# Issuing the stores of q*v from GpSimd's queue in place of SyncE's

## Chip, cores and metric

The kernel runs on one core of a Trainium2 chip. The metric is the device time of one execution in microseconds (us). The engines are TensorE (PE; its weight loads are PEld), VectorE (DVE), ScalarE (ACT), GpSimd (POOL) and SyncE (SP). SyncE computes nothing; it issues DMAs. The traces write a queue of a DMA-issuing engine as SPq, ACTq or POOLq.

## The reference

The reference is a chain of four layers on x of shape (8, 56, 56, 192) in float32. Each layer normalizes x in groups and adds its result to x. Layers 0 and 1, the only ones that the change touches, are these (layer 2 is a convolution block with an MLP, layer 3 windowed attention):

```python
x = gn(x)
p = silu(x @ p_w.T + p_b)
q = silu(x @ q_w.T + q_b)          # 192 -> 576 channels
v = silu(x @ v_w.T + v_b)
qv = q * v
o1 = toeplitz(qv along w, a1)      # one decaying filter per channel
o2 = toeplitz(qv along h, a2)
x = x + (p * (o1 + o2)) @ o_w.T + o_b
```

## The kernel before

Layers 0 and 1 each have three parts, and each part is run for two halves of the batch (j0 = 0 and j0 = 2):

- `tno_qv` computes q*v from x and stores it to the DRAM tensor `qv`.
- `tno_toeplitz` reads `qv` back and applies the two filters; its result goes to the DRAM tensor `L_sum`.
- `tno_out` computes p, multiplies it by that result, applies the output matrix and writes the next x.

`weave` runs `tno_toeplitz` of one half inside the loops of `tno_qv` or `tno_out` of other work: each of these is a generator that yields after a piece of work with an estimate of its time, and the weaver lets the Toeplitz generator take a step whenever its share is due. For example `tno_toeplitz` of the first half runs within the rest of `tno_qv` of that half and `tno_qv` of the second. The stretches of the trace in which `tno_qv` runs are about 0 to 960 us, 1330 to 1760 us and 2180 to 2620 us. From about 100 us on TensorE, ScalarE, VectorE and GpSimd execute in the order in which the program gives their instructions. SyncE executes its own queue in order as well, and waits where an instruction of it must wait.

In `tno_qv` a tile of 128 tokens is worked on in units of 512, 512 and 128 columns, or 512 and 128 where one call does a part of the columns. A unit has these steps:

1. TensorE multiplies into banks (L263).
2. VectorE adds the bias and writes a tile `z` (L272). `z` has three buffers ("t8").
3. In `multiply`, ScalarE applies silu to `z` (L301).
4. In `multiply`, GpSimd forms the product of its halves in a tile `prod` (L304). `prod` has three buffers ("t4"), which `tno_out` uses too.
5. The store of `prod` to `qv` (L307). It is not issued at once: it is put into the list `stores` and called at the start of the next `multiply`, ahead of the next silu and the next product.

A store of a 512-wide unit is 512 KB, in runs of 512 bytes, eight for each of 128 tokens. All stores together are 300.

In `tno_toeplitz` SyncE loads a block of q*v in the tile `q` (L380 along w, one of its two halves from ScalarE's queue; L383 along h) and the filter matrix `tm` (L393). TensorE multiplies (L406), ScalarE copies the result to `ot` (L413, two buffers), VectorE transposes it (L424 along w, straight into the sum `s`; L426 along h). In the half-step along h, GpSimd adds the transposed result to `s` (L429, four times in a half-step; on VectorE in the last block) and issues the stores of the sum (L436, or L444 in the last block) from its own queue. The other loads that SyncE issues in these stretches are x for `tno_qv` (L240), and x (L119) and sums (L508) for `tno_out`. In the first 440 us it also loads and stores what the filters are built from (L145 to L204).

Of the kernel before, what the change touches and what calls it, by code (L numbers as in the profile page):

```python
# [43 lines left out]
class Net:  # L44
# [179 lines left out]
    def tno_qv(self, L, j0, xs, gn, qv, apart=None, cols=(0, 2 * D1), g0=0):  # L224
# [3 lines left out]
        nc, p, inp = self.nc, self.tp, self.inp  # L228
# [68 lines left out]
        def multiply(m, n, z, at, c0):  # L297
            k = n // 128
            for f in stores:
                f()  # L300
            nc.scalar.activation(z[:m, :n, :], z[:m, :n, :], AF.Silu)  # L301
            prod = p.tile([128, 4, DC * 4], F32, name="t4")
            half = z[:m, :n, :].rearrange("p (n h c) b -> p n h (c b)", h=2, c=DC)
            nc.gpsimd.tensor_mul(prod[:m, :k], half[:, :, 0], half[:, :, 1])  # L304
            n0 = c0 // 128
            stores[:] = [
                lambda: nc.sync.dma_start(  # L307
                    qv[2 * n0 : 2 * n0 + 2 * k, at : at + m, :].rearrange("n t e -> t n e"),
                    prod[:m, :k].rearrange("p n (h e) -> p (n h) e", h=2),
                )  # L310
            ]
# [7 lines left out]
        if apart:  # L319
            units = []  # L320
            for g in range(2):
                x, t0, n = loaded[g]
                for s in range(0, n, 128):
                    for c0 in range(0, 2 * D1, 512):
                        k = min(512, 2 * D1 - c0)
                        z = apart.tile([128, k, 4], F32, name=f"z{len(units)}", bufs=1)
                        units.append((x, s, 128, c0, k, z, t0 + s))
            for j in range(2):
                for g in range(2):
                    normalize(*loaded[g], (j,))  # L330
                for x, s, m, c0, k, z, at in units:
                    if late is not None:
                        multiply(*late)
                    half_unit(x, s, m, c0, k, z, j)
                    if j:
                        late = (m, k, z, at, c0)
                        if len(loaded) < 4:
                            loaded.append(load(len(loaded)))
                    yield 2.7 * k / 512
            loaded = loaded[2:]  # L340
            normalize(*loaded[0])
        else:
            yield from self.all_norms()
            normalize(*loaded[0])
        for g in range(2 if apart else g0, groups):
            x, t0, n = loaded.pop(0)
            for s in range(0, n, 128):
                m = min(128, n - s)
                for c0 in range(*cols, 512):
                    k = min(512, cols[1] - c0)  # L350

                    if late is not None:
                        multiply(*late)
                    if c0 == max(cols[0], min(512, cols[1] - 512)) and s + 128 >= n and g + 1 < groups:
                        normalize(*loaded[0])
                    z = p.tile([128, 512, 4], F32, name="t8")
                    unit(x, s, m, c0, k, z)
                    late = (m, k, z, t0 + s, c0)
                    if c0 == cols[0] and s == 0 and g + 2 < groups:
                        loaded.append(load(g + 2))  # L360
                    yield 5.3 * k / 512
        multiply(*late)
        stores[0]()

# [1310 lines left out]
```

## Time and profile before

| what | value |
|---|---|
| median of 3 runs | 5452.3 us (5446.23 to 5452.5) |
| profiled execution, time | 5448.52 us |
| profiled execution, span from the first instruction to the last | 5446.5 us |
| mean granted TensorE clock | 0.978 |
| DMA moved | 1116.48 MB |
| GpSimd busy, whole span | 1767.5 us (32%) |
| product on GpSimd (L304) | 300 instructions, 550.08 us |
| GpSimd's adds (L429), 128 of them | 550.9 us |

A row of the groups names a line of the code, the engine, the operation, the tiles written and read, the number of instructions, their busy time and the mean of one in ns; behind the second bar stands the time that the engine was idle just before them and what ended it. A row of the waits gives the total in us, the number and the longest. A row of the timeline gives start and duration in us, and in brackets the idle time before it with what ended it. A mean granted clock of 1.00 is full speed. SyncE's instructions and the issuing of DMAs from ScalarE are not counted as busy time; a DMA issue on GpSimd has a row of its own.

### The profile page before, as it was taken

To read this page: it belongs to the slowest core of one execution; us is meant where nothing else is said; L and a number is where in the kernel's file an instruction comes from. 1 tells how busy PE (TensorE), PEld (TensorE's weight loads), DVE (VectorE), ACT (ScalarE), POOL (GpSimd) and SP (SyncE) were. 2 spreads that over 40 slices of the span, in tenths; PEclk is the share of its full clock that TensorE was granted. 3 is DMA by queue.
4 is the path that set the end of the run, shared out by engine and by line. 5 is a ranking of instruction groups with operands and counts; after the bars stand their busy time and mean duration, and the time that the engine had idled before them with its cause. 6 is when DMAs were issued, how large, how long until landed. Compare 5 with 4: busy or idle time off the path is not lost.

```text
span 5446.5 us, 144346 instructions
## 1 busy us (share of the span) xinstructions
PE 5166.3 (95%) x64672; PEld 3811.3 (70%) x64672; DVE 2588.6 (48%) x3990; ACT 2384.0 (44%) x3179; POOL 1767.5 (32%) x1291
## 2 busy tenths in 40 slices
PE   7879999999999999999999899989999999999998
PEld 4657777777777777777777778855665444777776
DVE  6535556455555555645566322422212331566665
ACT  3345555444554454655454322242323333444443
POOL 2225675233664333645443100000001100333333
PEclk9889999999999999999999999999999999999999
DMA  7699997887786999888897666634444221445442
GB/s 253 149 242 280 289 315 228 274 279 256 248 267 170 327 309 308 277 233 280 296 325 246 205 219 237 221 127 161 140 165 121 74 69 49 84 97 108 99 103 68
DMA packets 1051146, 1116.48 MB, mean 205 GB/s; under 512 B 235200, under 2 KB 986304, under 8 KB 1036128
## 3 DMA queue, kind: packets, MB, share of 16 engines
q1 hardware_dynamic: 911584, 854.88, 52.7%
q0 software_dynamic: 38144, 200.99, 9.6%
q10 hardware_dynamic: 100800, 51.38, 3.7%
q8 instruction: 508, 8.32, 0.6%
q14 instruction: 110, 0.90, 0.1%
HBM read 743.17 MB, written 363.94 MB: 203 GB/s over the span
## 4 chain that ended last, share of the span: by engine, by line
PE 49%; DMA 3%; DVE 2%; issue 1%; ACT 1%; POOL 1%; SPq 1%; ACTq 0%; POOLq 0%; DVEq 0%
PE bank L976 7%; PE bank L837 5%; PE bank L1056 5%; PE bank L1250 4%; PE bank L263 3%; PE bank L592 3%; PE bank L1070 3%; PE bank L536 3%; PE bank L1366 2%; PE bank L1280 2%; PE bank L1197 2%; PE bank L1321 2%; PE bank L586 1%; PE bank L406 1%; PE bank L1340 1%
## 5 line engine op out<-in xcount | busy, mean ns | idle before, releaser
L263 PE MATMUL bank<-wq,t 128*128 128x256 f32 (+4 forms) x7680 | 1289.1, 374 | 73.5 <-DVE t L272 43.7
L263 PEld LDWEIGHTS bank<-wq,t 128*128 128x128 f32 (+2 forms) x7680 | 1004.9, 190 | 351.6 <-issue 92.5
L272 DVE TENSOR_TENSOR t<-bank,wq 128x1024 f32<-128x1024 f32 (+3 forms) x480 | 517.7, 1112 | 691.4 <-PE bank L263 540.9
L304 POOL TENSOR_TENSOR t<-t 128x1024 f32<-128x1024 f32 (+2 forms) x288 | 528.4, 1848 | 673.9 <-ACT t L301 338.5
L413 ACT COPY ot<-bank 128x896 f32<-128x896 f32 x576 | 493.2, 909 | 511.5 <-PE bank L406 401.8
L429 POOL TENSOR_TENSOR s<-s,ot 128x1568 f32<-128x1568 f32 x128 | 550.9, 4305 | 197.4 <-DVE ot L426 137.7
L301 ACT ACTIVATE t<-t 128x2048 f32<-128x2048 f32 (+2 forms) x288 | 423.2, 1488 | 330.5 <-DVE t L272 320.5
L406 PE MATMUL bank<-q,tm 56*32 56x224 f32 x18432 | 505.1, 354 | 18.7 <-DMA tm<-L_tab 11.6
L406 PEld LDWEIGHTS bank<-q,tm 56*32 56x32 f32 x18432 | 340.2, 106 | 145.3 <-issue 84.1
L122 POOL DMA_DIRECT2D x<-t x112 | 87.0, 777 | 1087.6 <-DVE t L601 1022.9
L555 ACT ACTIVATE bank<-bank,wo 128x448 f32<-128x448 f32 x448 | 262.9, 606 | 386.2 <-PE bank L545 361.2
L560 DVE TENSOR_TENSOR t<-t,bank 128x896 f32<-128x896 f32 x224 | 242.7, 1087 | 397.8 <-ACT bank L555 339.8
L976 PE MATMUL bank<-z,w 128*128 128x448 f32 (+1 forms) x1344 | 414.4, 556 | 1.5 <-ACT h L985 1.5
L536 PE MATMUL bank<-t,wo 128*128 128x224 f32 x1792 | 372.0, 361 | 21.4 <-ACT t L515 10.2
L536 PEld LDWEIGHTS bank<-t,wo 128*128 128x128 f32 x1792 | 334.9, 192 | 51.0 <-issue 30.2
L592 PE MATMUL bank<-t,wo 128*128 128x224 f32 x1792 | 368.9, 359 | 0.0
L592 PEld LDWEIGHTS bank<-t,wo 128*128 128x128 f32 x1792 | 329.9, 190 | 31.2 <-issue 31.2
L837 PEld LDWEIGHTS bank<-xt,cm 113*112 113x112 f32 x3072 | 316.1, 180 | 42.8 <-issue 33.9
L837 PE MATMUL bank<-xt,cm 113*112 113x108 f32 (+2 forms) x3072 | 324.4, 265 | 10.8 <-ACT h L985 5.7
L976 PEld LDWEIGHTS bank<-z,w 128*128 128x128 f32 (+1 forms) x1344 | 183.0, 189 | 206.7 <-issue 198.7
L127 POOL DMA_DIRECT2D x<-x x64 | 36.7, 574 | 843.4 <-DVE x L1007 813.5
L424 DVE STREAM_TRANSPOSE s<-ot 128x1792 f32<-128x1792 f32 x144 | 292.8, 2034 | 23.0 <-ACT ot L413 14.8
(162 smaller groups left out, 6972.8 us busy)
## 6 DMA issues: line engine op xcount, KB each, us to landing
q<-qv SPq DMA_DIRECT2D x36, 3584.0 KB
t<-L_sum SPq DMA_DIRECT2D x112, 1008.0 KB
L_sum<-s POOLq DMA_DIRECT2D x256, 392.0 KB, 7.3
qv<-t SPq DMA_DIRECT2D x192, 512.0 KB
cm<-in_L_cm SPq DMA_DIRECT2D x96, 896.0 KB
tm<-L_tab SPq DMA_DIRECT2D x288, 240.0 KB
q<-qv SPq DMA_DIRECT2D x40, 1568.0 KB
q<-qv ACTq DMA_DIRECT2D x32, 1568.0 KB
```

The costliest lines, as they stand in the source:

```text
L263: nc.tensor.matmul(pp[:m, b, 256 * j : 256 * j + k], x[rows, j, 2 if part else b, s : s + m], w[rows, part, c0 + c : c0 + c + k],  start=p ...
L272: nc.vector.tensor_add(z[:m, c : c + k, :], view(pp[:m], 0, [[1, k], [256, 4]]), view(bias[:m], c0 + c, [[1, k], [0, 4]]),)
L301: nc.scalar.activation(z[:m, :n, :], z[:m, :n, :], AF.Silu)
L304: nc.gpsimd.tensor_mul(prod[:m, :k], half[:, :, 0], half[:, :, 1])
L406: nc.tensor.matmul(pt[32 * j : 32 * j + 32, r, hf * 224 : (hf + 1) * 224], tm[rows, at : at + 32], q[rows, :, 4 * c : 4 * c + 4], start=Tr ...
L413: nc.scalar.copy(view(ot, 4 * (g % 4), [[16, 2], [32, 112], [1, 4]]), view(pt, 0, [[512, 2], [4, 112], [1, 4]]),)
L424: nc.vector.transpose(to, of.rearrange("p (i k) -> p i k", k=32))
L429: add.tensor_add(to, to, view(of, 0, [[1, 28], [32, 56]]))
L536: mm(gs[c // 2][:, b, c % 2 * 256 : c % 2 * 256 + N], pw[:, 0, 128 * c : 128 * c + 128], xn[:, b], start=c % 2 == 0, stop=False,)
L592: mm(P[:, b, :N], ow[:, c, 0:128], g[:, 4 * b + c], start=False, stop=c == 3)
L837: nc.tensor.matmul(pc[:, 128 * e + 4 * m0 : 128 * e + 4 * m1], cm[:113, e, k, :], xt[:, m0 - 1 + k : m1 - 1 + k, c + e, :], start=n == 0 a ...
L976: nc.tensor.matmul(phs[c][:, s, :TT], w0[rows, part, at : at + 128], z[rows, Z[2 if part else s], :], start=part == flip, stop=part != flip,)
```

## The change

The store of `prod` is issued from GpSimd's queue instead of SyncE's, for all 300 units. The place of the call in the program is the same: at the start of the next `multiply`, or at the end of `tno_qv` for the last. The data, the shapes and the buffers are the same.

```diff
             nc.gpsimd.tensor_mul(prod[:m, :k], half[:, :, 0], half[:, :, 1])
             n0 = c0 // 128
             stores[:] = [
-                lambda: nc.sync.dma_start(
+                lambda: nc.gpsimd.dma_start(
                     qv[2 * n0 : 2 * n0 + 2 * k, at : at + m, :].rearrange("n t e -> t n e"),
                     prod[:m, :k].rearrange("p n (h e) -> p (n h) e", h=2),
                 )
```

## The prediction

> **What bounds the kernel now.** I read the page's busy times and its chain first, then the waits of the engines, then SyncE's own waits, then two stretches of the timeline.
>
> ```profile
> PE 5166.3 (95%) x64672; PEld 3811.3 (70%) x64672; DVE 2588.6 (48%) x3990; ACT 2384.0 (44%) x3179; POOL 1767.5 (32%) x1291
> PE 49%; DMA 3%; DVE 2%; issue 1%; ACT 1%; POOL 1%; SPq 1%; ACTq 0%; POOLq 0%; DVEq 0%
> ...
> POOL t L304 <- DMA qv<-t: 325.1, 58, 30.4
> DVE t L272 <- POOL t L304: 138.7, 37, 23.3
> PE bank L263 <- DVE t L272: 43.7, 14, 9.7
> ...
> SPq L307 <- POOL t L304: 698.6, 199, 23.7
> ```
>
> TensorE is busy 95% of the span, so the change can win only the time in which TensorE stands still for the store, and lose only by making it stand still anew. The three waits below form one chain: the product on GpSimd (L304) waits for an old store to give back its `prod` buffer (325.1 us), VectorE's bias add (L272) waits for the product to give back `z` (138.7 us), TensorE waits for L272 to empty a bank (43.7 us). At each step most of the wait is swallowed by slack. The last line says that SyncE stands at the store for 698.6 us until the product is there, with later loads behind it.
>
> The timeline shows why the store is late, in the worst place:
>
> ```profile
> 2545.05 0.70 SPq L380 DMA_DIRECT2D q<-qv  x1
> ...
> 2545.85 14.19 SPq L307 DMA_DIRECT2D qv<-t  x2
> ...
> 2564.56 3.02 POOL L304 TENSOR_TENSOR t<-t 128x1024 f32<-128x1024 f32 x2 [11.88 <-DMA qv<-t]
> ...
> 2566.93 0.69 DVE L272 TENSOR_TENSOR t<-bank,wq 128x512 f32<-128x512 f32 x1 [9.91 <-POOL t L304]
> ...
> 2567.67 2.93 PE L263 MATMUL bank<-wq,t 128*128 128x256 f32 x6 [9.67 <-DVE t L272]
> ```
>
> SyncE issues a load of q, and two stores right behind it take 14.19 us to issue where the tile view gives a median of 365 ns. The product waits 11.88 us, VectorE 9.91, TensorE 9.67. The same picture stands behind the q loads issued at 468, 581, 645, 1412 and 2385 us; after the first two, four `tm` loads (15.30 and 12.28 us) stand between as well.
>
> The other stretch shows GpSimd with no room left, in the half-steps of the Toeplitz part that add on GpSimd:
>
> ```profile
> 745.55 8.58 POOL L429 TENSOR_TENSOR s<-s,ot 128x1568 f32<-128x1568 f32 x2
> 754.42 2.11 POOL L436 DMA_DIRECT2D L_sum<-s  x4 [0.29 <-POOL s L429]
> 756.55 5.38 POOL L304 TENSOR_TENSOR t<-t 128x1024 f32<-128x1024 f32 x3
> 758.97 2.36 DVE L272 TENSOR_TENSOR t<-bank,wq 128x1024 f32<-128x1024 f32 x2 [1.14 <-POOL t L304]
> 761.47 6.79 PE L263 MATMUL bank<-wq,t 128*128 128x128 f32 x31 [1.92 <-ACT ot L413]
> ```
>
> From 741 to 762 us GpSimd runs without a pause, three products have piled up, and VectorE just begins to wait for them (1.14 us). Anything put on GpSimd here is seen by TensorE soon.
>
> **What the change takes away.** 300 issues leave SyncE. (a) The stalls of the chain above. From the timeline I took each TensorE gap over 0.7 us in the q/v stretches and kept those whose L272 waited for a product that waited for `qv<-t`: 2.85 us at 496, 3.39 at 610, 2.87 at 666, 1.91 at 1432, 2.08 at 2404, 9.67 at 2568. Sum 22.8 us. Gaps of 5.03 at 922, 5.16 at 1699 and 1.92 at 2326 lie behind VectorE's own adds of the last block (L429 on DVE) and stay. The 7.81 us at 2614, where L515 waits for a `t4` buffer, I leave in: the last store is issued late because the last product is, and it still has to land.
> (b) In the first 440 us SyncE's stores delay loads. At 292.83 two stores take 7.64 us and the x loads go out only at 300.56; TensorE waits 6.35 us for L246 on them, and 3.90 us for the small `wo` load that shares the queue. At 378 it waits 11.65 us for `tm`, whose loads left SyncE behind six stores (340 to 347 us) and a q load. I count 6.35 + 3.90 and half of 11.65 (the q load stays): 16 us.
> (c) The granted clock is 0.95 in 2400 to 2620 us, where the two longest waits lie, 1.00 in the undisturbed slices: 5% of 220 us is 11 us, and I count 3 for one of two waits gone. Total gain 42 us.
>
> **What it adds.** GpSimd issues 300 DMAs in its own order, between one product and the next. The trace has no GpSimd issue of this form, so I bound it by rows of the groups kept apart by form:
>
> ```profile
> L122 POOL DMA_DIRECT2D x<-t x112 | 87.0, 777 | 1087.6 <-DVE t L601 1022.9 <-DVE st L604 53.2 <-DVE t L523 7.9
> L127 POOL DMA_DIRECT2D x<-x x64 | 36.7, 574 | 843.4 <-DVE x L1007 813.5 <-DVE yn L939 27.5 <-issue 2.4
> L743 POOL DMA_DIRECT2D qv<-none x2 | 2.3, 1170 | 0.0
> ```
>
> By the code L127 moves 128 runs, L122 384 (128 rows of 3) and L743 2016 (112 rows of 18). The store of a 512-wide unit has 128 x 8 = 1024 runs of 512 B, that of a 128-wide one 256. Between L122 and L743 that gives 777 + 640/1632 x 393 = 0.93 us; between L127 and L122, 0.68 us. Ends: 0.57 (cheapest row) and 1.17 us (dearest). 200 x 0.93 + 100 x 0.68 = 254 us, plus up to 0.29 us where it directly follows its own product (as L436 does above): at most 341 us on an engine with 3679 us idle. So the mean costs nothing; what counts is the half-steps without room. A half-step of some 34 us holds about six products (91 in 520 us), so six stores: 4 x 0.93 + 2 x 0.68 and some 0.29s, 5 to 6.5 us. Walking the stretch above through with them put in, the adds end 2 us later, the first piled-up product 2.9 us later, the last 5 us; then come 15 us with little to do and GpSimd catches up. The row L429 counts 66 GpSimd adds in the q/v stretches (31, 16, 7, 12), four to a half-step: 16 half-steps. In most VectorE doesn't wait there today, or by under 1 us; so of 2.9 us I let 1.1 through: 16 x 1.1 = 18 us lost. Ends: 0 (all slack) and 5 (the last product's delay): 0 to 80 us.
>
> **Where the new store lands.** GpSimd's queue holds only stores, so no q load is ahead. The page's issues give 7.3 us for L436 (392 KB) and 7.4 us for L122 (336 KB) while DMA is 80 to 97% busy; scaled, 512 KB is about 10 us. `prod` has three buffers, so a store has two units, some 14 us, before it is missed. Behind four L436 (1.57 MB, about 6 us more) it may be just late, but there the product is late anyway. I count 0; if it took 20 us, today's stalls would stay.
>
> Two rules of the Trainium skill speak against this. The first is weighed at the 14.19 us row. "DMA: Bandwidth & Descriptors", section "Issuing engines are not separate DMA queues", says that all issuers share the same 16 engines and that another issuer saves only issue time. By it (a) stays, and the sum is 18 us lost less about 10 of (b): 5460. The row shows a queue that is full behind a 1.5 MB load, which is order and not bandwidth, so I follow the row. The second is weighed at L436: "SBUF — State Buffer", section "SBUF: two separate sides", says that some VectorE copies lock GpSimd out of writing descriptors and that SyncE's transfers are immune. At 741.10 four L436 took 2.10 us while VectorE ran L426 (741.66 to 745.6), no slower than the 2.11 at 754.42; L424, L426 and L272 don't do it. By the rule each store could lose the 2.0 us of a transpose, 300 x 2 = 600 us on GpSimd; I take 0, and keep it for the upper end.
>
> **Sum.** The profiled execution has a span of 5446.5 us and a time of 5448.5, within 0.1% of the median 5452.3, so I subtract from the median: 5452.3 - 42 + 18 = 5428 us.
>
> **Rivals.**
> 1. GpSimd becomes the bound of the add half-steps. Slower: break-even is 42/16 = 2.6 us per half-step reaching TensorE. At 5 us (a half-step's last product) it is 80 - 42 = 38 us slower, 5490. For it: the 1.14 us above, 98.5 us in which ScalarE's copy L413 already waits for L429. Against: half-steps at 580 and 700 us end with GpSimd waiting for ScalarE.
> 2. Gain and loss cancel: 5441 to 5463. For it: the gain is six gaps, the loss sixteen small ones.
> 3. It does not do what it says: the store lands as late on GpSimd's queue because the engines, not the queue, are full (DMA 1.00 in 500 to 600 us). Then only (b) and the loss remain: 5452 - 10 + 18 = 5460. Against: the landing times above.
>
> **Chances.** 0.2% is 11 us, about what a measurement can tell from no change. Forecast, 5392 to 5441: 0.60. Rivals 2 and 3 within 11 us: 0.15. Rival 1, with the tail of rival 3: 0.25. The forecast's own range is 5400 to 5441; to hold 8 in 10 the range takes in rival 2 and half of rival 1: 5395 to 5480.
>
> **What would show it.** Right: POOL L304 <- DMA qv<-t falls from 325 to under 60 us; the gaps at 496, 610, 666, 1432 and 2568 are gone; GpSimd's busy time rises by about 250 us; the row of the new issue is 0.9 us; DVE L272 <- POOL L304 has more, shorter waits. Wrong: an issue of 2 us or more; ACT L413 <- POOL L429 far above 98.5 us with TensorE gaps of 3 us or more in each add half-step; or waits for `qv<-t` still at 300 us.

## Result and profile after

| | before | after |
|---|---|---|
| median | 5452.4 us (4 runs, 5446.23 to 5456.65) | 5478.18 us (4 runs, 5468.96 to 5483.71) |
| ratio | | 1.0051 (95% interval 1.0038 to 1.0063) |
| profiled execution: time, span | 5448.52, 5446.5 us | 5468.96, 5466.8 us |
| mean granted TensorE clock | 0.978 | 0.974 |
| GpSimd busy | 1767.5 us | 2033.9 us |

The change makes the kernel slower by 26 us (21 to 34 by the interval), where 24 us faster was forecast. Ratios, here and below, are to the kernel before on the same chip. The page of the changed kernel, first its busy times, then the chain that ended last by engine:

```profile
PE 5179.8 (95%) x64672; PEld 3820.1 (70%) x64672; DVE 2591.8 (47%) x3990; ACT 2383.8 (44%) x3179; POOL 2033.9 (37%) x1591
PE 74%; POOL 6%; DMA 6%; DVE 5%; issue 4%; ACT 3%; SPq 1%; POOLq 0%; ACTq 0%; DVEq 0%
```

GpSimd has 266 us and 300 instructions more. The chain covers the whole span here and only 58% of it before, so these shares can't be set side by side. The waits (total in us, number, longest) say more. First two rows of the kernel before:

```profile
ACT ot L413 <- POOL s L429: 98.5, 34, 7.9
PE bank L536 <- ACT t L515: 10.2, 3, 7.8
```

Then the changed kernel:

```profile
ACT ot L413 <- POOL s L429: 155.4, 41, 10.8
DVE t L272 <- POOL t L304: 133.3, 38, 6.4
POOL t L304 <- DMA qv<-t: 84.0, 36, 5.1
POOL qv L307 <- POOL t L304: 59.7, 191, 0.9
PE bank L263 <- DVE t L272: 27.6, 16, 4.0
PE bank L536 <- ACT t L515: 19.9, 2, 10.1
```

The chain that the prediction wanted to cut is cut: the product waits 84.0 us for old stores where it waited 325.1, VectorE's longest wait for a product is 6.4 us and was 23.3, TensorE's wait for VectorE fell from 43.7 to 27.6 us. Two rows stand against that. ScalarE's copy L413 waits 155.4 us for GpSimd's adds (98.5 before). And in the last row TensorE stands twice, 10 us each time, for L515, the normalization of an x tile in `tno_out`. Before, this wait had one long stand, the 7.81 us at 2614 us that the prediction left in; the two of 10 us are at other places, where the prediction looked for no wait.

The issue itself cost what was estimated. The groups kept apart by form:

```profile
L307 POOL DMA_DIRECT2D qv<-t x300 | 258.3, 861 | 76.8 <-POOL t L304 59.7 <-issue 7.9 <-DMA qv<-t 3.1
```

258 us against 254, and the wait for the own product (59.7 us over 191 issues) is the 0.3 us of the L436 row.

The queue is not all that changed. Two DMA queues of the page (packets, MB, share of the 16 engines' span), first before, then after:

```profile
q1 hardware_dynamic: 911584, 854.88, 52.7%
q0 software_dynamic: 38144, 200.99, 9.6%
```

```profile
q1 hardware_dynamic: 680992, 739.26, 44.9%
q0 software_dynamic: 71168, 316.62, 16.2%
```

The 115.6 MB of the stores left q1 in 230592 packets of about 0.5 KB and came to q0 in 33024 of about 3.5 KB. What the larger packets are worth, apart from the queue, no run tells. In e7 below the stores keep the small packets on a third queue, and the product's wait for them is 140.1 us, far under 325.1 as well, though in a kernel that is held up elsewhere.

The place that the prediction showed first, where two stores took 14.19 us to issue behind a q load, looks like this in the timeline after (start, duration, in brackets the idle time before):

```profile
2568.29 0.33 SPq L380 DMA_DIRECT2D q<-qv  x1
2568.68 14.86 SPq L393 DMA_DIRECT2D tm<-L_tab  x4
...
2573.31 0.93 POOL L307 DMA_DIRECT2D qv<-t  x1 [0.30 <-POOL t L304]
2579.06 0.71 POOL L304 TENSOR_TENSOR t<-t 128x256 f32<-128x256 f32 x1 [4.82 <-DMA qv<-t]
```

The load is as before, and it is now the `tm` loads that stand 14.86 us in SyncE's queue behind it. The store is issued in its own 0.93 us, and what is left of the stall is smaller: the product still waits 4.82 us for a landing, and TensorE stands 3.51 us at 2581 in place of 9.67.

The other stretch, in an add half-step:

```profile
749.19 8.51 POOL L429 TENSOR_TENSOR s<-s,ot 128x1568 f32<-128x1568 f32 x2
...
757.73 1.71 ACT L413 COPY ot<-bank 128x896 f32<-128x896 f32 x2 [8.43 <-POOL s L429]
...
764.09 1.69 ACT L413 COPY ot<-bank 128x896 f32<-128x896 f32 x2
...
765.03 5.30 PE L263 MATMUL bank<-wq,t 128*128 128x128 f32 x24 [3.21 <-ACT ot L413]
```

The trace lags by 3.6 us here, and so do the two adds (749.19, 745.55 before). ScalarE waits 8.43 us for the first of them to free `ot`, its next copy comes at 764.09, and TensorE stands 3.21 us (1.92 before). Eight such gaps of 1.7 to 3.2 us are in the q/v stretches, 19.0 us together; before there is only this one of that size. A ninth, of 7.31 us at 2638 us, is no added loss: it stands where the 7.81 us for L515 stood at 2614 us. L515 doesn't wait there any more, and an add is late instead. All of TensorE's waits for L413 in front of L263, before and after:

```profile
PE bank L263 <- ACT ot L413: 5.9, 14, 1.9
PE bank L263 <- ACT ot L413: 17.3, 20, 3.2
```

**Where the time went.** I aligned the traces by ScalarE's instructions, which stand in one order in all kernels of the table below, and took the difference of their start times to the kernel before, as the median of nine neighbours. The table gives by how much that difference grew in a part. The part behind 2985 us (layers 2 and 3) is left out: no edit touches it, and it moved by -0.1 to +9.2 us from one kernel to another. The table sets single executions, on more than one chip, against one of the kernel before. How good a cell is shows in e11, which has the queues of the kernel before: outside the transitions its cells are 2.8, 4.1 and -2.7. So a cell is good to some 5 us, and the ratios decide on sums.

| kernel | startup, to 440 us | three q/v stretches | two transitions to `tno_out` | rest | at 2985 us |
|---|---|---|---|---|---|
| changed kernel | 6.5 | -5.0 | 18.1 | 0.6 | 20.2 |
| e1_startup_sync | 6.4 | 6.0 | 18.3 | 0.0 | 30.7 |
| e2_xn_in_place | 10.9 | 2.2 | 1.7 | 3.4 | 18.2 |
| e3_both | 5.2 | 1.8 | 1.0 | 3.9 | 11.9 |
| e4_filler | 10.2 | 37.0 | 4.1 | 2.4 | 53.7 |
| e5_sync_in_adds | 10.3 | -25.9 | 0.5 | 0.9 | -14.2 |
| e6_filler_behind | 3.9 | 27.5 | 2.9 | 0.9 | 35.2 |
| e9_sync_start_adds | 3.1 | -24.3 | 3.6 | -0.3 | -17.9 |
| e10_gpsimd_in_adds | 1.6 | 39.8 | 1.3 | 1.1 | 43.8 |
| e11_before_xn_late | 2.8 | 4.1 | 20.0 | -2.7 | 24.2 |

The q/v stretches, of which the prediction treats at length, are no slower in the changed kernel. The loss lies at the two transitions and, less clear of the 5 us, in the startup.

### The profile page after: what moved, and what is told of

The parts are those of the page before. It is cut to its first block, busy times and chain, and to the rows that moved or that the text cites. A ratio compares the mean times of both kernels' runs of the same rounds, so it can differ in the third digit from the quotient of the medians.

```text
span 5466.8 us, 144138 instructions
## 1 busy us (share of the span) xinstructions
PE 5179.8 (95%) x64672; PEld 3820.1 (70%) x64672; DVE 2591.8 (47%) x3990; ACT 2383.8 (44%) x3179; POOL 2033.9 (37%) x1591
## 4 chain that ended last, share of the span: by engine, by line
PE 74%; POOL 6%; DMA 6%; DVE 5%; issue 4%; ACT 3%; SPq 1%; POOLq 0%; ACTq 0%; DVEq 0%
PE bank L263 13%; PE bank L976 7%; PE bank L592 6%; PE bank L536 6%; PE bank L837 5%; PE bank L406 5%; PE bank L1056 5%; PE bank L1250 4%; DMA qv<-t 3%; PE bank L586 3%; PE bank L1070 3%; POOL t L304 3%; PE bank L545 2%; POOL s L429 2%; PE bank L1366 2%
## 5 line engine op out<-in xcount | busy, mean ns | idle before, releaser
L263 PE MATMUL bank<-wq,t 128*128 128x256 f32 (+4 forms) x7680 | 1292.6, 375 | 68.2 <-DVE t L272 27.6
L263 PEld LDWEIGHTS bank<-wq,t 128*128 128x128 f32 (+2 forms) x7680 | 1006.9, 190 | 348.2 <-issue 91.3
L272 DVE TENSOR_TENSOR t<-bank,wq 128x1024 f32<-128x1024 f32 (+3 forms) x480 | 517.7, 1112 | 691.8 <-PE bank L263 535.0
L413 ACT COPY ot<-bank 128x896 f32<-128x896 f32 x576 | 493.2, 909 | 540.4 <-PE bank L406 364.1
L429 POOL TENSOR_TENSOR s<-s,ot 128x1568 f32<-128x1568 f32 x128 | 551.3, 4308 | 203.2 <-DVE ot L426 137.2
L536 PE MATMUL bank<-t,wo 128*128 128x224 f32 x1792 | 373.6, 362 | 25.9 <-ACT t L515 19.9
L536 PEld LDWEIGHTS bank<-t,wo 128*128 128x128 f32 x1792 | 337.1, 193 | 54.8 <-issue 27.4
```

What stands on the lines that cost most here:

```text
L263: nc.tensor.matmul(pp[:m, b, 256 * j : 256 * j + k], x[rows, j, 2 if part else b, s : s + m], w[rows, part, c0 + c : c0 + c + k],  start=p ...
L272: nc.vector.tensor_add(z[:m, c : c + k, :], view(pp[:m], 0, [[1, k], [256, 4]]), view(bias[:m], c0 + c, [[1, k], [0, 4]]),)
L413: nc.scalar.copy(view(ot, 4 * (g % 4), [[16, 2], [32, 112], [1, 4]]), view(pt, 0, [[512, 2], [4, 112], [1, 4]]),)
L429: add.tensor_add(to, to, view(of, 0, [[1, 28], [32, 56]]))
L536: mm(gs[c // 2][:, b, c % 2 * 256 : c % 2 * 256 + N], pw[:, 0, 128 * c : 128 * c + 128], xn[:, b], start=c % 2 == 0, stop=False,)
```

## Experiments

**The transitions.** At 960 us in the changed kernel:

```profile
959.58 0.34 SPq L380 DMA_DIRECT2D q<-qv  x1
960.04 0.73 POOL L307 DMA_DIRECT2D qv<-t  x1 [0.30 <-POOL t L304]
970.82 1.50 ACT L515 ACTIVATE t<-t,gn 128x224 f32<-128x224 f32 x3 [8.86 <-DMA qv<-t]
971.44 4.10 PE L536 MATMUL bank<-t,wo 128*128 128x224 f32 x10 [10.13 <-ACT t L515]
```

L515 wants a "t4" buffer for the second x tile. It is the last but one product's, whose store (256 KB) was issued 0.46 us behind a q load and landed some 10.5 us later; the median of all stores is 6.5 us in the tile view of `qv`. At 1770 us it is the same (9.79 us). Before, L515 waited for nothing at this place:

```profile
954.98 1.49 ACT L515 ACTIVATE t<-t,gn 128x224 f32<-128x224 f32 x3
```

The addresses in the built programs tell why: in the kernel before, that tile has the buffer of the first x tile, which TensorE has just read; in the changed kernel it has the buffer of the last but one product. Which free buffer of the pool a tile gets is decided when the program is built, and moving the stores changed that decision. At the third transition, near 2614 us, the decision changed the other way: before, the second x tile had a product's buffer (the 7.81 us), now it has that of the first x tile. So there are two causes to tell apart, the late landing and the placing. e2_xn_in_place restores the placing and leaves all stores on GpSimd:

```diff
-        def normalize(j, x):
-            xn = p.tile([128, 3, N], F32, name="t4")
+        def normalize(j, x, xn=None):
+            xn = xn or p.tile([128, 3, N], F32, name="t4")
...
-            xn = normalize(*after) if after else None
+            xn = normalize(*after, None if before else xn) if after else None
```

> The changed kernel with all 300 stores on GpSimd, but at each transition from Q to O the second normalized x tile (L515) is written into the buffer of the first, as the kernel before has it placed, and not into that of the last but one product. Theory (the PE gaps of 10.13 us at 971 and 9.79 us at 1770 are a wait for that product's store, which the changed kernel's placing of buffers made): both gaps go, 18 to 20 us less than the changed kernel, 5458 to 5460. Rival 1 (GpSimd's store and the loads around it land late whatever waits for them): the gaps are then L406 or L536 waiting for q or for s instead, gain under 5 us. Rival 2 (GpSimd's own time is the loss): no gain, 5477 to 5479.

Measured: ratio to the kernel before 1.0026 (1.0016 to 1.0035), 14 us slower, where the changed kernel has 1.0051. The two transitions cost 1.7 us in place of 18.1. ScalarE's timeline at the same place:

```profile
969.60 1.49 ACT L515 ACTIVATE t<-t,gn 128x224 f32<-128x224 f32 x3
```

It waits for nothing. The theory holds: about half of the loss comes from this wait. (14 us above the kernel before is more than the 6 to 8 us expected; the startup and the q/v stretches of this execution are worse than the changed kernel's by 11.6 us in the table, without an edit there.)

The opposite, e11_before_xn_late: the kernel before, all stores on SyncE, with the changed kernel's placing.

```diff
+            self.prods = [*getattr(self, "prods", [])[-1:], prod]
...
+            last = self.prods[0].rearrange("p n c -> p (n c)")[:, : 3 * N].rearrange("p (k n) -> p k n", k=3)
-            xn = normalize(*after) if after else None
+            xn = normalize(*after, None if before or not woven else last) if after else None
```

> The kernel before with all stores on SyncE, and one edit: at each transition from Q to O the second normalized x tile is written into the buffer of the last but one product, where the changed kernel has it. Theory (the two gaps of 10 us are made by the placing of that tile, whoever begins the store): gaps of 8 to 10 us at L536 <- ACT L515 near 956 and 1750 us here too, 16 to 20 us above the kernel before. Rival (the store lands late only because GpSimd begins it behind the q load): SyncE's store is in time, 0 to 4 us above it.

Measured: 1.0020 (1.0013 to 1.0028), 11 us slower; the transitions cost 20.0 us in the table. TensorE's timeline of this kernel:

```profile
971.35 6.31 PE L537 MATMUL bank<-t,wo 128*128 128x224 f32 x16 [11.45 <-ACT t L516]
```

The gap is there with SyncE's stores too, at 956 us on the clock of the kernel before, and again ahead of 1773 us (L516 waits 9.53 us). So it comes with the placing, whoever begins the store. By the ratio it comes to less than the 16 to 20 us expected, and I don't explain that difference.

**The startup.** The products of the twelve first units fall into one stretch, and in the changed kernel GpSimd has no pause in it. GpSimd's timeline at the end of the stretch, first of the kernel before:

```profile
97.84 0.10 POOL L149 MEMSET L0pw<- 128x1 f32 x1
101.78 2.38 POOL L304 TENSOR_TENSOR t<-t 128x1024 f32<-128x1024 f32 x1 [3.84 <-issue]
```

Then of the changed kernel:

```profile
103.63 0.93 POOL L307 DMA_DIRECT2D qv<-t  x1 [0.30 <-POOL t L304]
104.58 0.74 POOL L304 TENSOR_TENSOR t<-z 128x256 f32<-128x256 f32 x1
105.24 0.11 POOL L149 MEMSET L0pw<- 128x1 f32 x1
```

The kernel before is done with these units and the first memset L149 by 97.94 us and then stands 3.84 us idle; the changed kernel gets to that memset at 105.24, 7.4 us later. The filter tables hang behind it on VectorE, and L272 behind those. e1_startup_sync gives the stores of these units back to SyncE, in fact of eleven: the twelfth is issued outside this loop, and the trace has 289 stores on GpSimd.

```diff
-        def multiply(m, n, z, at, c0):
+        def multiply(m, n, z, at, c0, by=nc.gpsimd):
...
-                        multiply(*late)
+                        multiply(*late, by=nc.sync)
                     half_unit(x, s, m, c0, k, z, j)
```

> The changed kernel, but the stores of the twelve units of the startup section are again begun by SyncE; the other 288 stay on GpSimd. Theory (the change loses in separate places: about 8 us in the startup, where GpSimd runs without a pause and each store's issue and the wait for its own product put off the memsets of the decay tables behind it; about 20 us at two transitions from Q to O; some 1 to 2 us in each of the add half-steps): 8 us less than the changed kernel, near 5470 us. Rival 1 (each GpSimd issue costs the same wherever it stands, 26 us over 300): 12 of 300 are worth 1 us, 5477. Rival 2 (the startup is bound by the loads, and what is won there is waited for again at tm<-L_tab at 386 us): 5476 to 5478.

Measured: 1.0039 (1.0026 to 1.0052), not separable from the changed kernel. The trace shows why: at 150 us the lag is 2.8 us in place of 8.5, but at 378 us it is 7.5 and 8.0. The later startup units have their stores on GpSimd still, and the lag is there again; that they make it is likely, and e9 below fits it. e3_both joins the two edits:

> Both edits together: the twelve startup stores by SyncE, and the second normalized x tile written into the first one's buffer; 288 stores on GpSimd. Theory: the two losses are in separate places and add, 26 to 28 us less than the changed kernel, 5450 to 5453, level with the kernel before; what then remains of the loss in the add half-steps (about 15 us) balances the removed stalls. Rival (one of the two only moves the wait): 5458 to 5470. That the removed stalls are worth the predicted 23 us net of the half-steps would be 5440 or less.

Measured: 1.0022 (1.0015 to 1.0029), 12 us slower than the kernel before. That can't be told from e2's 1.0026: the miss is the startup term, which these eleven stores don't decide.

**GpSimd's time without the queue.** e4_filler keeps SyncE's stores and puts a useless memset ahead of each product:

```diff
+            nc.gpsimd.memset(prod[:m, : 4 if k > 1 else 3], 0.0)
             half = z[:m, :n, :].rearrange("p (n h c) b -> p n h (c b)", h=2, c=DC)
```

> The kernel before with its stores on SyncE, and on GpSimd ahead of each product a memset of the product's tile (about 0.97 us for a unit 512 wide, 0.73 for one 128 wide, 300 in all, some 267 us), which computes nothing; the second normalized x tile is written into the first one's buffer, as the kernel before places it. It has the GpSimd time of the change without its queue. Theory: the startup loss of about 8 us and the half-steps' 10 to 18 us appear, the stalls of 23 us behind the q loads stay, no wait of 10 us at the transitions: 5465 to 5478, that is 13 to 25 us above the kernel before. Rival 1 (GpSimd's time is the whole of the loss, and more by what the removed stalls brought): 5490 to 5500. Rival 2 (GpSimd's time is hidden, the loss is the queue's): 5450 to 5456.

Measured: 1.0093 (1.0076 to 1.0109), 51 us slower, far over the theory's 13 to 25 and over the 38 to 48 of rival 1 too. But this filler lies between the landing of an old store and the product, and so makes each of today's stalls longer. e6_filler_behind has it where the change has its issue:

```diff
+        scr = p.tile([128, 256], F32, name="scr", bufs=1)
...
             for f in stores:
                 f()
+                for turn in range(3 if n > 128 else 2):
+                    nc.gpsimd.memset(scr, 0.0)
```

> The kernel before, stores on SyncE; on GpSimd, where the change issues the store, three memsets of 128x256 (two for a unit 128 wide) of a tile of their own that nothing reads, about 0.9 us, 300 times; second normalized x tile in the first one's buffer. Against e4_filler the filler no longer stands between the landing of an older store and the product. Theory (GpSimd's time as such costs some 45 us, and the move of the stores to another queue gives 30 of them back): 35 to 50 us above the kernel before. Rival (e4's 51 us was mostly the longer way from landing to product in the stalls behind the q loads, and the half-steps cost what was predicted): 15 to 25 us above it.

Measured: 1.0055 (1.0042 to 1.0067), 30 us slower, between the two expectations. The group of the filler, and a row of the waits:

```profile
L303 POOL MEMSET scr<- 128x256 f32 x782 | 244.4, 313 | 28.3
```

```profile
ACT ot L416 <- POOL s L432: 171.6, 42, 11.4
```

244 us of GpSimd time, about the dose of the change, raise ScalarE's wait for the adds from 98.5 to 171.6 us (L416 and L432 are L413 and L429 here) and cost 27.5 us in the q/v stretches, though the product's wait for stores even fell (245.0 us). So this time isn't hidden, at least while the stalls behind the q loads stay. The difference to e4, 21 us, I put down to the longer way from landing to product; no run takes that apart further.

**Half-steps apart from the rest.** e5_sync_in_adds has e2's edit, and lets SyncE issue the 105 stores that fall into the time in which adds are pending:

```diff
-                lambda: nc.gpsimd.dma_start(
+                lambda: (nc.sync if self.adding else nc.gpsimd).dma_start(
...
                     work += [(d, ot, ss[g // 4], g // 4, hf, blk) for hf in range(2)]
+                    self.adding = d == 1
...
                 d, ot, s, half, hf, blk = work.pop(0)
+                self.adding = d == 1 and bool(work)
```

> The changed kernel with the second normalized x tile in the first one's buffer, and the stores of q*v begun by SyncE while half-steps with adds are pending, by GpSimd otherwise (105 and 195 of 300). Theory (what is left of the loss, 14 us over the kernel before, is GpSimd's time in the add half-steps): it goes, time within 5 us of the kernel before, and the waits of L413 for L429 fall from 164 us to about 100. Rival 1 (the loss is spread over all units, products late for L272): still 8 to 12 us above the kernel before. Rival 2 (the q loads that fall into these windows hold SyncE's stores up again): 15 us or more above it, with new gaps of 3 us or more at L263 <- DVE L272.

Measured: 0.9981 (0.9974 to 0.9987), 10 us faster than the kernel before. Its waits:

```profile
ACT ot L414 <- POOL s L430: 91.4, 34, 11.2
POOL t L305 <- DMA qv<-t: 66.6, 30, 6.6
```

Both sides are there at once: ScalarE waits for the adds no more than before the change (91.4, 98.5), and the product hardly waits for stores (66.6, 325.1). The 195 stores that GpSimd issues outside the half-steps are enough to remove the stalls. e2 and e5 were run on one chip and differ in the 105 stores alone: 1.0026 against 0.9981, some 24 us (16 to 33 by the intervals). The complement, e10_gpsimd_in_adds, differs only in the two queues being swapped:

> The complement of e5_sync_in_adds: GpSimd begins only the 105 stores that fall into the time in which half-steps with adds are pending, SyncE the other 195; second normalized x tile in the first one's buffer. Theory (the half-steps are where GpSimd's issues cost, and the stores elsewhere are where they gain): 15 to 30 us above the kernel before, L413 waiting for L429 some 150 us, the stall gaps of before at 496, 610 and 666 us still there. Rival (a GpSimd issue costs and gains the same anywhere): a third of what e2 showed, 3 to 8 us above it.

Measured: 1.0063 (1.0051 to 1.0076), 34 us slower, more than expected, and more than e2 with all 300 stores on GpSimd (1.0026). Its waits:

```profile
POOL t L305 <- DMA qv<-t: 305.1, 52, 32.4
ACT ot L414 <- POOL s L430: 199.7, 46, 12.0
```

The stalls stay (305.1) and the half-steps get worse (199.7). So these 105 alone are worse than all 300. A likely reason, not tested, is that a product late from its half-step now meets stores held up in SyncE's queue. Rival 1 of the prediction is thus half right: GpSimd becomes a bound of the half-steps, but 24 us over 16 of them are 1.5 us each, under the 2.6 at which it would outweigh the predicted gain.

**Other queues.** e7_stores_by_scalar issues all stores from ScalarE, e8_q_by_scalar leaves them on SyncE and moves the q loads to ScalarE; both have e2's edit.

```diff
+            nc.scalar.activation(z[:m, :n, :], z[:m, :n, :], AF.Silu)
             for f in stores:
                 f()
-            nc.scalar.activation(z[:m, :n, :], z[:m, :n, :], AF.Silu)
...
-                lambda: nc.sync.dma_start(
+                lambda: nc.scalar.dma_start(
```

```diff
-                    by = nc.scalar if half and n > 1 else nc.sync
+                    by = nc.scalar if n > 1 else nc.sync
...
-                nc.sync.dma_start(q.rearrange("p i e -> p (i e)"), of)
+                by = nc.scalar if n > 1 else nc.sync
+                by.dma_start(q.rearrange("p i e -> p (i e)"), of)
```

> The kernel before, with the stores of q*v begun by ScalarE behind the next unit's Silu in place of SyncE; nothing is added on GpSimd; second normalized x tile in the first one's buffer. Theory (the queue is worth 25 to 30 us once GpSimd's time isn't paid for it): 20 to 28 us less than the kernel before, if ScalarE rarely waits for a product. Rival (ScalarE's queue is in order: in the half-steps with adds the product is 4 to 9 us late, and L413 and the next Silu wait behind the store): 10 to 40 us more than the kernel before, with gaps of L406 and L263 waiting for L413.

> The kernel before, stores of q*v on SyncE, but all loads of q after the first two begun by ScalarE (before: half of every second load); second normalized x tile in the first one's buffer. Theory (SyncE's stores are held up by the q loads ahead of them in SyncE's own queue): the waits of the product for a store fall from 325 us to under 150, 15 to 25 us less than the kernel before. Rival (the loads hold up the stores wherever they are begun, by their share of the DMA engines; or SyncE is held up by the loads of the matrices, which stay): within 5 us of it, waits still near 300.

Measured: 1.0311 (1.0297 to 1.0325) and 1.0314 (1.0300 to 1.0328), both some 170 us slower. A row of the waits of e7, one of its tile view of qv and one of e8's tile view of q (with the min, median and max of the issue in ns):

```profile
ACT ot L413 <- POOL t L304: 123.4, 26, 12.5
L307 ACTq DMA_DIRECT2D qv<-t x300: 365/367/18785, 73.9 to 2769.7; - x150
```

```profile
L380 ACTq DMA_DIRECT2D q<-qv x64: 313/2922/13812, 400.2 to 3039.3; - x64
```

In e7 the rival came true, and much larger than thought: ScalarE waits for a product in front of its copy (123.4 us) and in front of the next x tile (91.6 us for L246), and one issue of a store holds it for up to 18.8 us. In e8 ScalarE itself stands in the issue of a q load, 2.9 us in the median and up to 13.8, where its 32 issues before took 0.3 us: an engine that computes now stands where SyncE stood. Neither theory nor rival of e8 had that. The product still waits 278.3 us for stores, so e8 doesn't settle whether order in SyncE's own queue is the whole of the stall.

**The best version.** e9_sync_start_adds is e5 with the startup's stores on SyncE as well (151 by GpSimd):

```diff
+        self.adding = True
...
         NS = 2 * (D1 // DC)
+        self.adding = False
```

> As e5_sync_in_adds, and the stores of the whole startup (up to the first Toeplitz step) by SyncE as well: 151 of 300 by GpSimd. Theory (in the profile of e5 the startup still loses some 10 us to the kernel before, and all of it is GpSimd's time; behind the startup e5 gains some 24 us): near 5430 us where the kernel before has 5453, a ratio of 0.995 to 0.997. Rival 1 (the lag of the startup is made up for later anyway, since the Toeplitz stretch then starts behind loads that are no earlier): as e5, 0.998. Rival 2 (with SyncE's stores the first stall gaps come back at the start of the stretch): 0.998 to 1.000.

Measured: 0.9963 (0.9949 to 0.9977), 20 us faster than the kernel before and in the expected interval. The startup loses 3.1 us in place of 10.3. It beats the kernel before and the changed kernel; from e5 (0.9974 to 0.9987) the ratio doesn't separate it.

## Why the prediction was wrong

The sign was wrong: 24 us faster was forecast, 26 us slower measured, 50 us apart. The startup term makes some 22 of them, the transitions 18, the half-steps most of the rest. Step by step:

- **The path and gain (a) with (c): right, nearly whole.** Five of the six gaps are gone, and the largest is 3.51 us in place of 9.67. The product's wait for stores is 84.0 us, not under 60. The clock in the stretch of the longest waits rose from 0.95 to 0.98. The sum was 22.8 + 3 = 25.8 us; e5 and e9, in which the stores outside the half-steps moved, gain 25.9 and 24.3 us there, as near as the table can tell. The 7.81 us at 2614 us were rightly left in as a sum, but not for the reason given: L515's wait went, and a late add took its place (7.31 us).
- **The issue: right.** 258 us against 254; 0.629 to 0.975 us an issue, within the ends named.
- **The half-steps, 18 us: right in kind, at the low end in size.** With the stores of the half-steps on GpSimd, the changed kernel, e1, e2 and e3 stand at -5.0 to +6.0 us in the q/v stretches; without them e5 and e9 stand at -25. So these stores cost 20 to 31 us by the table, 24 by the ratios of e2 and e5, whose intervals (16 to 33) don't exclude 18. Of the marks for "wrong" the first half came, L413's wait far above 98.5 us; the gaps are mostly smaller than the mark and stand in half of the 16 half-steps.
- **Startup (b), a gain of 16 us: the first step that failed.** "I count 6.35 + 3.90 and half of 11.65" took delays of loads as time won, and put no cost on GpSimd, which was looked at for the half-steps only. The startup lost 6.5 us. The 3.90 us are gone, but 5.39 of the 6.35 remain, TensorE waits 12.91 us for `tm` where 11.65 was to be halved, and new gaps of 2.99 and 4.48 us stand at 113 and 125 us. With SyncE's stores in the startup (e9, e10, e11) the loss is 1.6 to 3.1 us, with GpSimd's (the changed kernel, e2, e5) 6.5 to 10.9, so it comes from the stores on GpSimd. How much is time on GpSimd stays open: the two fillers cost 3.9 and 10.2 us there.
- **"I count 0" for the landing: the second step that failed,** but not as feared. For 512 KB the landing was estimated at 10 us, and the page has a median of 6.9. The step asked only who in `tno_qv` waits for a store. The last products' buffers are next used by `tno_out`, and the rebuilt program gave its second x tile the wrong one of them at two of three transitions: 18.1 us in two gaps. e2 takes it away, e11 makes it on SyncE. Rival 3, a store as late on GpSimd's queue, isn't the cause. That the placing would change could not be read from the trace before.

With the measured terms the sum is 18 + 6.5 - 25.8 + 20 to 31 = 19 to 30 us; the medians give 26. As the terms come from one table, this shows that no large term is missing, not that each is right.

The two rules of the Trainium skill that were weighed: that another issuer only saves issue time ("DMA: Bandwidth & Descriptors", "Issuing engines are not separate DMA queues") would, as the prediction read it, leave the product's wait near 325 us; it fell to 84.0, so for this stall the row was the better guide. At the transitions the shared engines of that rule fit: a 256 KB store 0.46 us behind a q load took some 10.5 us to land, with the DMA share at 1.05. That some of VectorE's operations lock GpSimd out of writing descriptors ("SBUF — State Buffer", "SBUF: two separate sides") wasn't seen: no issue of 300 took over 0.975 us. But the section names operations in a 2-port mode, and does not say that the transposes here are such, so the 600 us of the prediction were not that rule's, and it wasn't put to the test.

## What to carry to other kernels

When a transfer is moved to another queue, compare where the rebuilt program puts the tiles that share its pool, first of all where one stage hands over to the next; here this cost 18 us where 24 were to be won. Move the transfers only where the new issuer has room: issuing on an engine that computes is paid for in the stretches where it has no room, and a version that chooses the queue by stretch kept the gain and skipped the price. A delay found in a loaded startup is no gain until the work that then bounds it is named.

## What the runs showed of the hardware

A long stand costs more than its own time. By stretch, in and after the gap that ends at 971.4 us (busy times of PE, PEld, DVE, ACT and POOL, the granted clock, DMA share, GB/s):

```profile
960.00:971.40 11.40, 1.31 (x12) 0.39 (x8) 2.17 (x2) 2.48 (x6) 2.11 (x3) 0.66 1.05 181
971.40:980.00 8.60, 8.56 (x42) 7.02 (x44) 0.39 (x1) 2.52 (x6) 0.00 (x0) 0.65 1.03 318
980.00:1000.00 20.00, 20.00 (x138) 16.88 (x138) 7.00 (x12) 7.07 (x14) 0.77 (x1) 1.00 1.09 284
```

The mean clock is 0.66 over the stand, 0.65 in the next 9 us and 1.00 behind them. In e2, which doesn't stand there, it is 1.00 all through:

```profile
962.00:980.00 18.00, 16.81 (x125) 13.15 (x123) 4.28 (x5) 10.35 (x17) 6.97 (x6) 1.00 0.77 136
```

In e11 the first sixteen L536 after its gap take 6.31 us, where the sixteen ahead of it take 3.29.
